# Layer norm's factor as exp(-0.5 ln(var + eps)), with one activation table set for the whole kernel

## Chip, cores, metric

The kernel runs on one core of a Trainium2 chip. The metric is the device time of one execution in microseconds (us), medians of several executions. A trace belongs to one execution; its span is some 1.8 us shorter than the time. A span is printed to 0.1 us, so lengths that run to its end are good to 0.05 us.

## The reference, cut to what matters

```python
def _layernorm(x, axis=-1, eps=1e-5):
    m = jnp.mean(x, axis=axis, keepdims=True)
    v = jnp.var(x, axis=axis, keepdims=True)
    return (x - m) / jnp.sqrt(v + eps)

# x: 64 graphs x 256 nodes x 512 features, adj: 64 x 256 x 256, all float32
x = _layernorm(x + relu(concat([x, adj @ x / deg]) @ W.T))            # layer 0
w = inv_scale * mask * rowsum((x @ Wq) * (adj @ (mask * (x @ Wk))))
x = _layernorm(x + softmax(w, axis=nodes)[:, :, None] * (x @ Wv))     # layer 1
```

Two norms for each graph, 128 in all, and one softmax over the nodes of each graph. The kernel does the softmax for two graphs at once, 32 times.

## The kernel before

The kernel is software-pipelined: round i does layer 0 of graph i, layer 1 of graph i-2, and finishes graph i-4. Its products use a seven-multiplication block scheme; their helper is line L155, the products with the adjacency are L254. A scheduler decides the order on each engine from the program's dependencies and its own estimate of the times, so that a changed instruction can also move others.

```python
    def transpose_rows(src, dst):            # x1 -> x1T, for the products of layer 1
        ...
        for t in range(NT):
            nc.vector.transpose(sq[:, :, :, t, :].rearrange("p b c q -> p c b q"), src[:, t, :])
        ...
        for a in range(P // Q):
            for b in range(P // Q):          # 16 transfers, issued one after the other
                nc.sync.dma_start(to[b * Q:(b + 1) * Q, :, a, :], ...)

    def layer_norm(src, dst):
        mv = small.tile([P, NT, 2], F32, name="mv")
        for t in range(NT):
            st = small.tile([P, 6], F32, name="st")
            nc.vector.bn_stats(st, src[:, t, :])
            nc.vector.bn_aggr(mv[:, t, :], st)
        rstd = small.tile([P, NT], F32, name="rstd")
        nc.scalar.activation(rstd, mv[:, :, 1], AF.Sqrt, bias=eps)      # L180
        nc.vector.reciprocal(rstd, rstd)                                # L181
        for t in range(NT):                                             # L183
            nc.vector.tensor_scalar(dst[:, t, :], src[:, t, :], mv[:, t, 0:1], rstd[:, t:t + 1],
                                    op0=OP.subtract, op1=OP.mult)
    ...
    def norm0(g):                            # end of layer 0
        layer_norm(owns.pop(g), x1s[g])
        for t in range(NT):                  # masked copy for the adjacency product of the next round
            nc.scalar.activation(values(g + 1)[:, 1, t, :], x1s[g][:, t, :], AF.Copy,
                                 scale=mask_sb[:, t, g:g + 1])
        transpose_rows(x1s[g], x1Ts[g])
    ...
    def softmax_rows(k):
        ...
        wr = ps_tp.tile([G, NT, P], F32, name="tp")
        for t in range(NT):
            nc.tensor.transpose(wr[:, t, :], w[:, t, :], ident)         # L349
        nc.vector.reduce_max(top, wr.rearrange("g t p -> g (t p)"), axis=AX.X)
        nc.vector.tensor_scalar(top, top, -1.0, None, op0=OP.mult)      # L352
        nc.scalar.activation(e, wr, AF.Exp, bias=top, accum_out=total)  # L355
        nc.vector.reciprocal(total, total)
        nc.vector.tensor_scalar(e, e, total, None, op0=OP.mult)
        return e
    ...
    def finish(g):
        for t in range(NT):
            nc.vector.scalar_tensor_tensor(o[:, t, :], v[:, t, :], p[:, t, g % G:g % G + 1], x1[:, t, :],
                                           op0=OP.mult, op1=OP.add)     # L371
        layer_norm(o, o)
        nc.sync.dma_start(out[g].rearrange("(t p) f -> p t f", p=P), o)
```

The square root and the exponential lie in different table sets of ScalarE, so each softmax brings two table loads: the exponential's, and the square root's for the next norm. A table load (ACT_TABLE_LOAD) is put in wherever the needed function isn't in the loaded set.

## Time and profile before

| | before |
|---|---|
| median of 3 runs (later, of 6) | 2003.67 us (2003.88 us) |
| span of the profiled run | 2002.7 us |
| TensorE (PE) busy | 1971.7 us, 98% |
| VectorE (DVE) busy | 1526.0 us, 76% |
| ScalarE (ACT) busy | 677.8 us, 34% |
| of that, table loads | 66, of 1.283 us each |
| granted clock of TensorE, mean | 0.995 |

Read it from the top: a kernel whose TensorE is busy for 98% of the span can lose time to another engine only where TensorE waits for it. The prediction shows where that is: at the start, and in the last 60 us, when the pipeline drains and no other graph's work covers a wait.

### The profile page before, as it was taken

The page shows a single profiled execution, that of the slowest core. Times are in us where ns is not written, and L with a number is a line of the kernel's source. Part 1 is how long each engine was busy: PE and PEld are TensorE (multiplying, and loading weights), DVE is VectorE, ACT ScalarE, POOL GpSimd, SP SyncE. Part 2 cuts the span into 40 slices and gives each one's busy share as a digit, 9 for nine tenths or more (in the row PEclk, how much of TensorE's full clock was granted, in tenths as well). Part 3 has the DMA queues.
Part 4 walks back from the last instruction along what each step waited for, and adds up shares of the span by engine and source line. Part 5 has one row for each costly group of instructions (what it writes and reads, how often), then busy time and mean ns, then how long its engine had stood idle before and what let it go on. Part 6 is the DMA issues. An engine that isn't in the chain of part 4 may idle for free.

```text
span 2002.7 us, 19342 instructions
## 1 busy us (share of the span) xinstructions
PE 1971.7 (98%) x5536; PEld 1030.1 (51%) x5536; DVE 1526.0 (76%) x3184; ACT 677.8 (34%) x1354; POOL 418.0 (21%) x518
## 2 busy tenths in 40 slices
PE   8999999999999999999999999999999999999995
PEld 3555555555555555555555555555555555555552
DVE  4677778777788777787777787777877777877776
ACT  2333333333333333333333333333333333333322
POOL 3122122221221221221222212212212212222100
PEclk9999999999999999999999999999999999999998
DMA  6333332333333333333323323323233333233211
GB/s 221 85 79 78 96 90 74 91 89 84 90 79 92 94 75 94 90 75 99 90 76 89 93 78 92 89 82 92 73 95 90 78 96 90 73 91 92 60 38 53
DMA packets 384905, 174.40 MB, mean 87 GB/s; under 512 B 283809, under 2 KB 349473, under 8 KB 384801
## 3 DMA queue, kind: packets, MB, share of 16 engines
q1 hardware_dynamic: 384800, 173.17, 32.6%
q8 instruction: 46, 0.75, 0.2%
q14 instruction: 59, 0.48, 0.1%
HBM read 105.97 MB, written 33.55 MB: 70 GB/s over the span
## 4 chain that ended last, share of the span: by engine, by line
PE 97%; DVE 1%; SPq 0%; ACT 0%; DMA 0%; issue 0%; DVEq 0%; ACTq 0%
PE mm L155 77%; PE mm L254 19%; PE mm L126 1%; SPq L170 0%; PE tp L363 0%; PE tp L349 0%; DMA wqk<-wqk_t 0%; DVE st L177 0%; DVE o L371 0%; ACT L355 0%; DVE own L286 0%; DVE own L288 0%; DMA x1T<-sq 0%; DVE o L183 0%; ACT vals L295 0%
## 5 line engine op out<-in xcount | busy, mean ns | idle before, releaser
L155 PE MATMUL mm<-w,s 128*128 128x512 f32 x1024 | 481.3, 592 | 0.7 <-ACT v L325 0.7
L155 PE MATMUL mm<-t,s 128*128 128x512 f32 x1024 | 464.9, 596 | 0.6 <-ACT q L318 0.6
L155 PEld LDWEIGHTS mm<-t,s 128*128 128x128 f32 x1024 | 192.4, 190 | 231.1 <-issue 214.0
L155 PEld LDWEIGHTS mm<-w,s 128*128 128x128 f32 x1024 | 194.5, 190 | 192.6 <-issue 170.0
L155 PE MATMUL mm<-w,x1T 128*128 128x512 f32 x512 | 242.6, 596 | 4.1 <-DMA x1T<-sq 4.1
L155 PE MATMUL mm<-w,xT 128*128 128x512 f32 x512 | 240.9, 592 | 0.0
L196 POOL TENSOR_TENSOR sa<-adj 128x128 f32<-128x128 f32 x64 | 45.8, 715 | 773.7 <-PE mm L254 772.2
L147 POOL TENSOR_TENSOR s<-xT 128x256 f32<-128x256 f32 x64 | 46.5, 726 | 704.4 <-PE mm L155 684.7
L254 PE MATMUL mm<-tv,sa 128*128 128x256 f32 x768 | 187.4, 379 | 0.6 <-DVE tv L244 0.4
L254 PEld LDWEIGHTS mm<-tv,sa 128*128 128x128 f32 x768 | 145.7, 190 | 76.3 <-issue 60.3
L155 PEld LDWEIGHTS mm<-w,xT 128*128 128x128 f32 x512 | 97.3, 190 | 94.7 <-issue 91.3
L333 DVE TENSOR_TENSOR v<-mm,v 128x512 f32<-128x512 f32 x64 | 44.2, 691 | 127.5 <-ACT v L332 127.5
L286 DVE SCALAR_TENSOR_TENSOR own<-zr,rdeg,own 128x512 f32<-128x512 f32 x128 | 107.6, 841 | 42.4 <-ACT zr L276 42.4
L155 PEld LDWEIGHTS mm<-w,x1T 128*128 128x128 f32 x512 | 95.3, 191 | 86.0 <-issue 74.8
L325 ACT COPY v<-mm 128x512 f32<-128x512 f32 x64 | 37.4, 585 | 299.6 <-PE mm L155 299.6
L314 DVE SCALAR_TENSOR_TENSOR q<-mm,zr 128x512 f32<-128x512 f32 x128 | 87.6, 684 | 66.7 <-PE mm L155 66.6
L155 PE MATMUL mm<-t,x1T 128*128 128x512 f32 x256 | 125.5, 612 | 0.7 <-ACT v L332 0.7
L254 PE MATMUL mm<-vals,adj 128*128 128x256 f32 x512 | 121.3, 379 | 1.9 <-DVE vals L228 1.9
L155 PE MATMUL mm<-t,xT 128*128 128x512 f32 x256 | 120.5, 593 | 2.4 <-ACT vals L217 2.4
L371 DVE SCALAR_TENSOR_TENSOR o<-v,probs,x 128x512 f32<-128x512 f32 x128 | 120.2, 958 | 0.1
L254 PEld LDWEIGHTS mm<-vals,adj 128*128 128x128 f32 x512 | 97.1, 190 | 43.6 <-issue 20.8
L210 ACT COPY own<-mm 128x512 f32<-128x512 f32 x64 | 37.4, 585 | 227.5 <-PE mm L155 227.5
(83 smaller groups left out, 2676.4 us busy)
## 6 DMA issues: line engine op xcount, KB each, us to landing
xT<-x_t SPq DMA_DIRECT2D x64, 512.0 KB, 4.3
x<-x SPq DMA_DIRECT2D x64, 512.0 KB, 3.6
x1T<-sq SPq DMA_DIRECT2D x1024, 32.0 KB, 2.0
out<-o SPq DMA_DIRECT2D x64, 512.0 KB, 2.9
adj<-adj_t SPq DMA_DIRECT2D x64, 256.0 KB, 2.7
rows<-adj SPq DMA_DIRECT2D x64, 256.0 KB, 4.9
wqk<-wqk_t SPq DMA_DIRECT2D x4, 512.0 KB, 5.2
w<-w_t SPq DMA_DIRECT2D x4, 512.0 KB, 9.2
```

Of the source, the lines that this page charges most:

```text
L126: nc.tensor.matmul(ps[c], wqk[:, a, c * P:(c + 1) * P], wqk[:, NA + a, :], start=(a == 0), stop=(a == NA - 1))
L147: eng.tensor_add(s1, a21, a22)
L155: nc.tensor.matmul(ps, a[:, c, :], b[:, c, :], start=start and c == 0, stop=(c == H - 1), skip_group_check=True)
L196: nc.gpsimd.tensor_add(sa[:, 0], a21, a22)
L210: began = nc.scalar.copy(own[:, 0, :], u)
L254: nc.tensor.matmul(ps[:, k * HF:(k + 1) * HF], sumsA[g - k][a], w[b][:, n, :], start=start and n == 0, stop=True, skip_group_check=True)
L286: nc.vector.scalar_tensor_tensor(own[:, t, :], z[:, t, :], rdeg[:, t:t + 1], own[:, t, :], op0=OP.mult, op1=OP.add)
L314: nc.vector.scalar_tensor_tensor(q, a, 1.0, agg[:, t, :], op0=OP.mult, op1=OP.mult, accum_out=to)
L325: nc.scalar.copy(v[:, 0, :], u)
L333: nc.vector.tensor_add(v[:, 1, :], p5, v[:, 1, :])
L371: nc.vector.scalar_tensor_tensor(o[:, t, :], v[:, t, :], p[:, t, g % G:g % G + 1], x1[:, t, :], op0=OP.mult, op1=OP.add)
```

## The change

The intent: get rid of all table loads but one, and of the reciprocals. 1/sqrt(v) is exp(-0.5 ln v), and one table set holds both ln and exp. It is loaded at the start and serves the softmax too.

```diff
+    nc.scalar.preload_act_table_set("natural_log_exp_and_others")
     const = ctx.enter_context(tc.tile_pool(name="const", bufs=1))
@@ layer_norm
-        nc.scalar.activation(rstd, mv[:, :, 1], AF.Sqrt, bias=eps)
-        nc.vector.reciprocal(rstd, rstd)
+        nc.scalar.activation(rstd, mv[:, :, 1], AF.Ln, bias=eps)
+        nc.scalar.activation(rstd, rstd, AF.Exp, scale=-0.5)
```

From here on, a line number of the changed kernel is larger by one than that of the kernel before (L156 for L155); the experiments' own edits shift theirs a little more.

## The prediction

> **What bounds the kernel now.** I read the page first (share of the span of each engine), then the chain that ended last, then the waits of TensorE, then the busy time by stretch, and last the timeline of the tail.
>
> ```profile
> PE 1971.7 (98%) x5536; PEld 1030.1 (51%) x5536; DVE 1526.0 (76%) x3184; ACT 677.8 (34%) x1354; POOL 418.0 (21%) x518
> ...
> PE 97%; DVE 1%; SPq 0%; ACT 0%; DMA 0%; issue 0%; DVEq 0%; ACTq 0%
> ```
>
> TensorE (PE) is busy for 1971.7 of 2002.7 us, and the chain is 97% matmuls. Only 31 us of the span are not matmuls; nothing that leaves the matmuls alone can win more than that. The waits of TensorE say where these 31 us lie (us in total, times, longest):
>
> ```profile
> PE mm L126 <- DMA wqk<-wqk_t: 4.5, 1, 4.5
> PE mm L155 <- DMA x1T<-sq: 4.1, 1, 4.1
> PE tp L363 <- DVE e L357: 3.6, 1, 3.6
> PE mm L155 <- ACT vals L217: 2.4, 2, 1.7
> ...
> PE mm L155 <- ACT v L325: 0.7, 1, 0.7
> PE mm L155 <- ACT v L332: 0.7, 1, 0.7
> PE mm L155 <- ACT q L318: 0.6, 1, 0.6
> ```
>
> Nearly every one happens once, so they belong to the start and the tail, not to the 64 rounds. The stretches confirm it (window, its length, then busy time of PE, PEld, DVE, ACT, POOL, then granted clock and DMA):
>
> ```profile
> 62.62:1944.19 1881.57, 1881.57 (x5309) 986.80 (x5309) 1458.12 (x3042) 644.40 (x1286) 400.47 (x488) 1.00 0.33 85
> ```
>
> From 62.62 to 1944.19 us TensorE is busy all 1881.57 us at full clock. The layer norms in there can't be seen in the time.
>
> What the change touches, from the groups of instructions:
>
> ```profile
> L180 ACT ACT_TABLE_LOAD x33 | 42.3, 1283 | 0.6
> L355 ACT ACT_TABLE_LOAD x32 | 41.1, 1283 | 34.4 <-DVE top L352 34.4
> L180 ACT ACTIVATE rstd<-mv,eps 128x2 f32<-128x2 f32 x128 | 37.8, 295 | 95.7 <-DVE mv L178 94.3
> L181 DVE RECIPROCAL rstd<-rstd 128x2 f32<-128x2 f32 x128 | 19.4, 151 | 8.0 <-ACT rstd L180 8.0
> ```
>
> Each softmax (L355, one per two graphs) loads the exponential's table and the next norm (L180) loads the square root's back: 65 loads, 83.4 us of ScalarE, plus one at the very start. It looks like 4% of the span, but ScalarE is 34% busy and waits mostly for TensorE.
>
> **What the Trainium skill says.** "ScalarE: Activation LUTs", section "What ACT_TABLE_LOAD costs": about 1283 ns per load, the same for every set, and about 1380 ns of drain at each switch. The trace agrees on 1283 ns; it shows no drain as a gap: in the last softmax the load starts at 1987.92, and the exponential at 1989.22, 0.02 us after it ends. I count 1.28 us per load. Section "Table sets: the hidden batching unit" of that page: exp and ln are together in natural_log_exp_and_others, so one load serves both. The trace before can't show that; the changed program, built and listed, holds one load in place of 66. The page's cost of an ACTIVATE (186 ns with immediate scale and bias, 93 ns for each pointer operand, 0.83 ns per element) makes the new Exp on 2 columns 0.19 us, 0.28 if the zero bias goes by pointer; the trace has 0.295 for the Sqrt with a pointer bias, so I use 0.2 to 0.3. "TensorE: Matmul & The Clock Gate", section "What's actually happening": the array falls to half clock after an idle window of some 3.4 us. The trace agrees: in the one wait for x1T in the tail the clock drops, and the next 3.5 us run at 0.50:
>
> ```profile
> 1966.90:1970.99 4.09, 0.00 (x1) 0.03 (x1) 3.23 (x10) 0.29 (x1) 0.00 (x0) 0.77 0.39 91
> 1970.99:1974.50 3.51, 3.51 (x4) 1.48 (x5) 1.49 (x4) 0.00 (x0) 0.00 (x0) 0.50 0.67 247
> 1974.50:1978.60 4.10, 4.10 (x9) 1.81 (x8) 0.70 (x2) 0.59 (x1) 0.00 (x0) 0.83 0.00 0
> ```
>
> **The change part by part, middle.** Removed: 65 loads (83.4 us of ACT) and 128 reciprocals (19.4 us of DVE). Added: 128 Exp on ACT (26 to 38 us, an estimate from the 0.2 to 0.3 us above). Ln takes Sqrt's place at the same 0.295 us. So ACT should fall from 678 to 622 to 634 us and DVE from 1526 to about 1507. I compared the two built programs. TensorE's order is the same but for a handful of matmuls in the last rounds; GpSimd's is the same. On VectorE the steady order moves a little: one pair of output scalings (L183, 1.0 us) now precedes the add that frees a PSUM bank (L265), where a reciprocal and two other additions stood. Nothing here precedes a matmul that waits. Worth in the middle: 0 us. At the start (45 to 50 us) the first load ends at 46.69, before its statistics are there (mv at 46.82), so it is hidden: 0 us.
>
> **The tail, where it can count.** Two places have a load on the path.
>
> First, the softmax at 1951 us. The load of 1.28 us holds the copy of q, the next load holds the norm of the last graph, and this norm decides when x1T starts to be transposed:
>
> ```profile
> 1951.30 1.28 ACT L355 ACT_TABLE_LOAD   x1 [3.83 <-DVE top L352]
> ...
> 1953.64 1.28 ACT L180 ACT_TABLE_LOAD   x1
> 1953.67 1.12 PE L155 MATMUL mm<-t,s 128*128 128x512 f32 x2 [0.59 <-ACT q L318]
> ...
> 1956.64 1.00 DVE L183 TENSOR_SCALAR x<-own,mv,rstd 128x512 f32<-128x512 f32 x2
> ...
> 1958.91 10.40 SPq L170 DMA_DIRECT2D x1T<-sq  x16
> ```
>
> With the order of the changed program I replay it with these durations. The exponential runs at 1951.26 and is read out by 1951.9; statistics (L177, L178) and the small softmax product end at about 1953.95; Ln and Exp take 0.6 us to 1954.6, beside the dot product of 0.75 us that VectorE does meanwhile; L183 starts at 1954.75, not 1956.64: 1.9 us earlier. The 16 transposing transfers start 1.9 us after that start, are issued serially in 10.4 us, and TensorE waited 4.09 us for the last. It therefore resumes 1.9 us earlier, at about 1969.1. Gain 1.9 us.
>
> TensorE's own work before it starts about when it did (1956.7, now waiting for the masked copy) and ends near 1966.7, so its wait shrinks to 2.2 to 2.6 us. In the trace before, a mean clock of 0.77 over 4.09 us, if it was first 1.00 and then 0.50, means that the clock fell 2.2 us into the wait. So it is even whether the shorter wait still costs the half clock. If not, the 4 matmuls take 1.88 and the next 8 take 3.60 in place of 3.75 and 4.28: 2.5 us. At even odds I count 1.3 us.
>
> Second, the last softmax: its load (1987.92, 1.28 us) stands between the maximum and the exponential with nothing beside it. Gain 1.28 us. The load after it is hidden: the last norms' Sqrt starts at 1994.51, as soon as its statistics are there.
>
> Given back: at the very end the changed order scales the graph before the last before it takes the last statistics; the last Ln and Exp are then exposed, 0.6 us, where before the scaling covered Sqrt and reciprocal. The first of the two outputs leaves earlier and doesn't share the DMA with the last: 0.1 us back.
>
> Sum: 1.9 + 1.3 + 1.28 - 0.6 + 0.1 = 4.0 us. 2003.7 - 4.0 = 1999.7 us.
>
> **The rivals.** (a) The loads count in full: 83 us of ACT less 32 of Exp, so some 50 us and 1953 us, if ScalarE paced the rounds. Against it: the stretch of 1881.57 us without a gap, and TensorE's busy time of 1971.7 us, that is not touched. I give it 1%. (b) A new wait takes their place: Ln and Exp now stand in ScalarE's in-order queue ahead of a PSUM copy, and the L183 pair delays L265. Each round two copies are close: the matmul after L332's copy starts as soon as it ends. Should a round lose 0.3 us, it would be 64 x 0.3 = 19 us, 2019 us. Against it: Ln and Exp take 0.6 us where load and Sqrt took 1.58, and where no load was they take 0.3 more, with the copy's wait for TensorE mostly above 0.8 us. 4%. (c) The tail's gain is hidden: TensorE or VectorE, not x1T, ends the wait, as VectorE is over 90% busy there. Then only the 1.28 - 0.6 us of the end remain: 2003 us. 20%. (d) My replay with the cold clock kept: 2001.0; with it warm: 1998.5.
>
> **Range and chances.** From (d), with 1.5 us for the spread of the three runs before (2001.9 to 2005.0), and (c) at its upper end: 1997.0 to 2002.8. 2% is 40 us, more than all of the time that isn't matmuls: faster 0.01, slower 0.01, within 0.98.
>
> **What would show it.** One load in the list of groups; ACT near 628, DVE near 1507, PE within 3 us of 1971.7 unless the tail's clock stays up; the middle still without a wait; L183 of the last graph starting some 1.9 us nearer to the start of its softmax; a wait for x1T of 2 to 3 us; the last exponential directly after L352. Wrong: a wait of TensorE for ACT or DVE that comes some 30 or 60 times, or a wait for x1T that is unchanged.

## The result

| | before | after |
|---|---|---|
| median (lowest to highest), 6 runs each | 2003.88 (2001.94 to 2004.99) us | 2000.26 (1998.14 to 2002.65) us |
| span of the profiled run | 2002.7 us | 1996.4 us |
| TensorE busy | 1971.7 us | 1968.4 us |
| VectorE busy | 1526.0 us | 1514.0 us |
| ScalarE busy | 677.8 us | 628.1 us |

The ratio is 0.9984 (95% interval 0.9971 to 0.9996). A ratio is the mean time of one kernel's fast runs over that of the other's of the same rounds, so it is not quite the ratio of the medians. The change is real and small: 3.6 us between the medians, of 85 us of table loads. The profiled run of the changed kernel happens to be its fastest of six, and that of the kernel before (2004.58 us) is slower than its median, so the two traces lie further apart (6.3 us) than the medians.

The page of the changed kernel, and its groups that answer to the four shown before (count, then busy us and mean ns, then idle time ahead):

```profile
PE 1968.4 (99%) x5536; PEld 1029.0 (52%) x5536; DVE 1514.0 (76%) x3056; ACT 628.1 (31%) x1417; POOL 411.1 (21%) x518
...
L181 ACT ACTIVATE rstd<-mv,eps 128x2 f32<-128x2 f32 x128 | 37.8, 295 | 110.8 <-DVE mv L179 108.1
L182 ACT ACTIVATE rstd<-rstd 128x2 f32<-128x2 f32 x128 | 26.0, 203 | 4.0
...
L69 ACT ACT_TABLE_LOAD x1 | 1.3, 1283 | 0.7 <-PEq L431 0.7
```

One load is left; the new Exp takes 203 ns. ScalarE lost 49.7 us of work, and the time fell by 3.6. The same stretch in the middle as before, and TensorE's waits within it (us, times, longest):

```profile
62.62:1944.19 1881.57, 1881.06 (x5307) 986.71 (x5306) 1446.22 (x2918) 600.47 (x1348) 392.19 (x486) 1.00 0.33 85
...
PE mm L156 <- ACT vals L218: 0.5, 1, 0.5
```

Before, TensorE was busy for all of this stretch; now it waits once, for 0.5 us. So nothing was won in the middle. What is left is the start and the tail. I cut the span at events that all versions share:

- start: the first product of layer 0 begins at 20.96 us before and at 20.14 after. In eleven traces it begins between 19.99 and 21.23 us, in no relation to the edits, which leave the matmuls ahead of it as they are. I don't credit these 0.8 us to the change.
- middle: from there to the last regular product (`mm<-t,x1T`, at 1944.03 and 1943.46 us), 1923.07 us before and 1923.32 after: 0.25 us lost.
- tail: from there to the end, 58.67 us before and 52.94 after: 5.73 us won.

The tail by sections, in us:

| section of the tail | before | after | difference |
|---|---|---|---|
| (1) to the first matmul after the wait for x1T | 26.96 | 24.74 | -2.22 |
| (2) to the transposes of the last scores (L349) | 15.47 | 13.03 | -2.44 |
| (3) to the first product with the last softmax (L371) | 4.59 | 3.23 | -1.36 |
| (4) to the last pair of scalings (L183) | 6.47 | 7.03 | +0.56 |
| (5) to the end of the span | 5.18 | 4.91 | -0.27 |

The timeline of the changed kernel in section (1) (start, duration, engine, line; in brackets the idle time ahead and what ended it):

```profile
1950.75 0.47 ACT L356 ACTIVATE e<-tp,top 2x256 f32<-2x256 f32 x1 [3.84 <-DVE top L353]
...
1953.12 0.29 ACT L181 ACTIVATE rstd<-mv,eps 128x2 f32<-128x2 f32 x1 [1.35 <-DVE mv L179]
...
1953.44 0.20 ACT L182 ACTIVATE rstd<-rstd 128x2 f32<-128x2 f32 x1
...
1953.68 1.00 DVE L184 TENSOR_SCALAR x<-own,mv,rstd 128x512 f32<-128x512 f32 x2
...
1955.96 10.39 SPq L171 DMA_DIRECT2D x1T<-sq  x16
...
1968.20 1.96 PE L156 MATMUL mm<-w,x1T 128*128 128x512 f32 x4 [2.31 <-DMA x1T<-sq]
```

The exponential starts without a load ahead of it, the norm's factor follows as soon as its statistics are there, and the last graph is scaled 10.22 us after the last regular product (1953.68 - 1943.46); before, it was 12.61 (1956.64 - 1944.03). The transposing transfers start as much earlier, and TensorE's wait for them shrinks from 4.09 to 2.31 us. After it the four matmuls take 1.96 us, where they took 3.75 at half clock.

Not all of these 2.39 us can be put down to the loads. The same place in the kernel before, from the square root on:

```profile
1954.93 0.30 ACT L180 ACTIVATE rstd<-mv,eps 128x2 f32<-128x2 f32 x1
...
1955.24 0.75 DVE L371 SCALAR_TENSOR_TENSOR o<-v,probs,x 128x512 f32<-128x512 f32 x1
1955.91 0.16 DVE L181 RECIPROCAL rstd<-rstd 128x2 f32<-128x2 f32 x1
1955.99 0.73 DVE L371 SCALAR_TENSOR_TENSOR o<-v,probs,x 128x512 f32<-128x512 f32 x1
```

ScalarE was done with the square root 11.20 us after the last regular product (1955.23 - 1944.03), and is done with Exp after 10.18 (1953.64 - 1943.46): 1.02 us. The other 1.37 us lie on VectorE. From there to the start of the scaling 1.41 us passed before, with the reciprocal between two instructions that finish an earlier graph (L371), and 0.04 us after, where those two (L372) come behind the scaling. Loads, reciprocal and order changed together, and no run parts them.

Section (3), the timeline of the kernel before and that of the changed one:

```profile
1987.70 0.14 DVE L352 TENSOR_SCALAR top<-top 2x1 f32<-2x1 f32 x1
1987.92 1.28 ACT L355 ACT_TABLE_LOAD   x1 [5.06 <-DVE top L352]
1989.22 0.46 ACT L355 ACTIVATE e<-tp,top 2x256 f32<-2x256 f32 x1
```

```profile
1982.47 0.14 DVE L353 TENSOR_SCALAR top<-top 2x1 f32<-2x1 f32 x1
1982.71 0.46 ACT L356 ACTIVATE e<-tp,top 2x256 f32<-2x256 f32 x1 [5.07 <-DVE top L353]
```

The load's place is simply gone. Section (4), from the chain that ended last in the changed kernel (start, duration, what):

```profile
1990.67 0.23 DVE mv L179 x2
1990.90 0.02 issue
1990.92 0.30 ACT rstd L181
1991.23 0.02 issue
1991.25 0.21 ACT rstd L182
1991.46 0.03 issue
1991.49 0.55 DVE o L184
```

Statistics, Ln, Exp and the scaling follow each other with nothing beside them. That is the half microsecond that was given back.

### The profile page after: what moved, and what is told of

It is laid out like the page before. It is cut to its first block, busy times and chain, and to the rows that moved or that the text cites. A ratio compares the mean times of both kernels' runs of the same rounds, so it can differ in the third digit from the quotient of the medians.

```text
span 1996.4 us, 19070 instructions
## 1 busy us (share of the span) xinstructions
PE 1968.4 (99%) x5536; PEld 1029.0 (52%) x5536; DVE 1514.0 (76%) x3056; ACT 628.1 (31%) x1417; POOL 411.1 (21%) x518
## 4 chain that ended last, share of the span: by engine, by line
PE 96%; DVE 2%; SPq 1%; DMA 0%; ACT 0%; issue 0%; DVEq 0%; ACTq 0%
PE mm L156 76%; PE mm L255 19%; SPq L171 1%; PE mm L127 1%; PE tp L364 0%; PE tp L350 0%; DVE st L178 0%; DMA xT<-x_t 0%; DMA wqk<-wqk_t 0%; DVE own L289 0%; DVE own L287 0%; DVE o L372 0%; ACT vals L296 0%; DVE x L184 0%; DMA x1T<-sq 0%
## 5 line engine op out<-in xcount | busy, mean ns | idle before, releaser
L156 PE MATMUL mm<-w,s 128*128 128x512 f32 x1024 | 481.2, 592 | 0.0
L156 PE MATMUL mm<-t,s 128*128 128x512 f32 x1024 | 463.9, 595 | 0.0
L156 PEld LDWEIGHTS mm<-t,s 128*128 128x128 f32 x1024 | 192.1, 190 | 229.2 <-issue 213.6
L156 PEld LDWEIGHTS mm<-w,s 128*128 128x128 f32 x1024 | 194.6, 190 | 191.1 <-issue 162.6
L156 PE MATMUL mm<-w,x1T 128*128 128x512 f32 x512 | 240.8, 593 | 2.3 <-DMA x1T<-sq 2.3
L156 PE MATMUL mm<-w,xT 128*128 128x512 f32 x512 | 240.9, 592 | 0.0
L229 DVE TENSOR_TENSOR vals<-mm,vals 128x512 f32<-128x512 f32 x64 | 44.3, 692 | 134.6 <-PE mm L156 134.6
L156 PEld LDWEIGHTS mm<-w,xT 128*128 128x128 f32 x512 | 97.3, 190 | 94.6 <-issue 91.3
L156 PEld LDWEIGHTS mm<-w,x1T 128*128 128x128 f32 x512 | 94.8, 190 | 83.7 <-issue 79.4
L156 PE MATMUL mm<-t,x1T 128*128 128x512 f32 x256 | 125.5, 612 | 0.9 <-ACT v L333 0.7
L156 PE MATMUL mm<-t,xT 128*128 128x512 f32 x256 | 120.6, 593 | 2.8 <-ACT vals L218 2.8
L372 DVE SCALAR_TENSOR_TENSOR o<-v,probs,x 128x512 f32<-128x512 f32 x128 | 118.4, 963 | 0.0
```

Of the source, the lines that this page charges most:

```text
L156: nc.tensor.matmul(ps, a[:, c, :], b[:, c, :], start=start and c == 0, stop=(c == H - 1), skip_group_check=True)
L229: nc.vector.tensor_add(y[:, 0, :], p5, y[:, 0, :])
```

## The experiments

Theory: the gain lies in the tail alone, in three terms (the last graph's norm earlier, TensorE's clock, the last softmax's load), less what the exposed Ln and Exp at the end give back. Rivals: the middle's relief of ScalarE and VectorE brings it; the clock isn't the cause of the slow matmuls; the spread is all there is to see. All results were correct against the reference. All were timed in 5 rounds but for the last, in 3; the kernel before ran along, with medians of 2004.21, 2003.51 and 2003.15 us in the three sessions.

### Ln and Exp in the tail alone, and in the middle alone

```diff
-        nc.scalar.activation(rstd, mv[:, :, 1], AF.Ln, bias=eps)
-        nc.scalar.activation(rstd, rstd, AF.Exp, scale=-0.5)
+        if at_round[0] >= 62:              # tail_only;  < 62 in middle_only
+            nc.scalar.activation(rstd, mv[:, :, 1], AF.Ln, bias=eps)
+            nc.scalar.activation(rstd, rstd, AF.Exp, scale=-0.5)
+        else:
+            nc.scalar.activation(rstd, mv[:, :, 1], AF.Sqrt, bias=eps)
+            nc.vector.reciprocal(rstd, rstd)
```

(In tail_only the shared set is loaded ahead of the exponential of round 62, in middle_only at the start.)

> Ln and Exp with the shared set only from round 62 on (the last softmax but one, the norms of the last graphs); square root, reciprocal and 61 loads in all rounds before. My theory (the gain lies in the tail alone): the tail from the last regular rounds to the end takes about 53 us as in the changed kernel, not 58.7 as in the kernel before, the middle keeps its loads and shows no wait, and the time is within 1.5 us of the changed kernel's 2000.3. Rival (the middle's relief of ScalarE and VectorE brings the gain): the time stays at that of the kernel before, 2003.9.

> The complement: Ln and Exp with the shared set up to round 61, square root, reciprocal and five loads from round 62 on. My theory: 60 loads and over 110 reciprocals less in the middle bring nothing; the tail takes about 58.7 us as before, and the time is 2003.9 within 1.5 us (or 0.5 to 0.8 us worse, for the one new wait of TensorE for the copy to vals near 70 us). Rival: most of the gain of 3.6 us is here, about 2000.5.

Measured: tail_only 1998.29 us (1997.40 to 2000.24), ratio to before 0.9972 (0.9959 to 0.9984). middle_only 2004.38 us (2003.11 to 2005.38), ratio 1.0001 (0.9988 to 1.0013). The tail takes 52.94 us in tail_only, as in the changed kernel, and 60.08 in middle_only. The stretch from 62.62 us to the last regular product, first in tail_only, then in middle_only (columns as before: PE, PEld, DVE, ACT, POOL, then clock and DMA):

```profile
62.62:1943.46 1880.84, 1880.84 (x5308) 986.19 (x5306) 1458.93 (x3038) 644.26 (x1287) 398.35 (x487) 1.00 0.33 85
```

```profile
62.62:1943.32 1880.70, 1880.19 (x5306) 985.61 (x5304) 1445.20 (x2921) 601.43 (x1345) 397.47 (x486) 1.00 0.33 85
```

With all its loads and 43 us more of ScalarE's work, tail_only's TensorE never waits in the middle; relieved, that of middle_only waits the same 0.5 us as in the changed kernel. The rival falls: 59 loads and over 110 reciprocals less in the middle gain nothing, and the new order costs a little there. (tail_only's 2 us below the changed kernel's median of six is more than the middle explains; it is outside the 1.5 us that I expected. They ran on different occasions, and I take no more from it than that it isn't slower.)

### The clock: the wait filled with useless matmuls

```diff
+        if i == B + 1:
+            warm = bank()
+            for _ in range(4):
+                nc.tensor.matmul(warm, ident, w0[:, 0, :], start=True, stop=True, skip_group_check=True)
         l1 = layer1_steps(i - 2) if 0 <= i - 2 < B else iter(())
```

> The kernel before with four useless matmuls (about 3.4 us) that run in the tail's wait for x1T. My theory (2.4 us of the changed kernel's gain is TensorE's clock, which no longer falls to half because the wait is short): from the first matmul after the wait to the transposes of the last scores 13.0 us, not 15.5, granted clock 1.00 there, nothing else moves, 2001.5 us. Rival (those 12 matmuls are slow for another reason, such as the row sums or the transfers): 15.5 us stay, 2003.9 us.

Measured: 2002.63 us (2002.26 to 2005.56), ratio 0.9995 (0.9982 to 1.0009), so the time alone would not settle it. The sections do: 27.97, 13.03, 4.60, 6.46 and 5.11 us. Section (2) is 13.03 us, to the hundredth that of the changed kernel, with the same norms and loads as before:

```profile
1966.33 3.60 PE L400 MATMUL mm<-w,ident 128*128 128x512 f32 x8
1971.60 1.96 PE L155 MATMUL mm<-w,x1T 128*128 128x512 f32 x4 [1.68 <-DMA x1T<-sq]
```

The matmuls after the wait take 1.96 us. That the 2.44 us of section (2) are the clock's is shown, and the rival falls. Section (1) was 1 us longer here than in the profiled run of before. It is 27.6 to 28.0 us in the three other traces with the old tail, and 24.7 to 25.6 in the traces with the new one: the 16 transfers' issue takes 10.4 to 11.4 us from one execution to the next. The profiled run of before was a lucky one in this section. Why the issue varies stays open.

### The last load alone

```diff
+        if k == B // G - 1:
+            tc.keep_in_program_order(nc.scalar.preload_act_table_set("exp_and_others"))
         wr = ps_tp.tile([G, NT, P], F32, name="tp")
```

> The kernel before with the exponential's table for the very last softmax loaded some 4 us earlier, while ScalarE is idle; every load is still there. My theory (of 65 loads this is one of the two that cost): from the transposes of the last scores to the first product with the softmax 3.3 us, not 4.6; all else as before; 2002.6 us. Rival (the load there is hidden by the read-out and the waits around it): 4.6 us stay.

Measured: 2002.19 us (2001.42 to 2003.44), ratio 0.9991 (0.9979 to 1.0004). Section (3) is 3.23 us, as in the changed kernel, where it was 4.59. The timeline of this kernel:

```profile
1982.53 1.28 ACT L348 ACT_TABLE_LOAD   x1
...
1987.58 0.46 ACT L357 ACTIVATE e<-tp,top 2x256 f32<-2x256 f32 x1 [3.77 <-DVE top L354]
```

The same load, five microseconds earlier, is free. It is its place that cost 1.36 us. Not all else was as before, though: section (2) took 14.73 us in place of 15.47, since the clock was at half for 3.41 us and not for 6.83. So the sections show the load's cost; the 2.0 us between the medians hold more than the load, and the interval of the ratio reaches beyond 1.

### The changed kernel again, and with the last scalings held back

> The changed kernel once more, on the chip of the next two. 2000 us within 1.5; the tail 52.9 us when the clock stays up and about 55.4 when it falls; again one wait of 0.5 us near 70 us that the kernel with Ln and Exp in the tail alone hasn't.

Measured: 1999.23 us (1998.93 to 2000.30), ratio 0.9980 (0.9967 to 0.9992); tail 53.89 us, sections 25.62, 13.03, 3.32, 7.03, 4.89. The wait for x1T was 3.19 us here, and the clock held. From the first product to the last regular one it took 1923.75 us. In the five traces with Ln and Exp from the start on this is 1923.32 to 1923.77 us; in the six with the old rounds it is 1923.06 or 1923.07 in five, and 1922.62 in one.

For end_order the statistics and the scaling of a norm were made separate functions, and `finish` uses them:

```diff
-        layer_norm(o, o)
-        nc.sync.dma_start(out[g].rearrange("(t p) f -> p t f", p=P), o)
+        mv = small.tile([P, NT, 2], F32, name="mv")
+        stats(o, mv)
+        held.append((g, o, mv, factor(mv)))       # factor: Ln and Exp
+        if g == B - 2:
+            return
+        for h, o, mv, rstd in held:
+            scaled(o, o, mv, rstd)
+            nc.sync.dma_start(out[h].rearrange("(t p) f -> p t f", p=P), o)
+        held.clear()
```

> The changed kernel, with the scaling of the last two graphs held back until both have their statistics, so that other work covers the last Ln and Exp, as the kernel before covered its last square root. My theory (0.56 us were given back because the last Ln and Exp stand exposed): from the first product with the last softmax to the last scaling 6.2 to 6.5 us, not 7.0, and 0.6 us less in all, or a little less because both outputs then leave together. Rival (the last stretch is bound by VectorE's own work or the output's transfer): no change in the span.

Measured: sections (4) and (5) 6.45 and 5.14 us, against 7.03 and 4.91. So the 0.56 us are the exposed pair's, as expected, and 0.23 us go back, probably because both outputs leave together. But the time was 2002.54 us (1998.30 to 2003.10), in two clumps: 1998.3 and 1999.4, and 2002.5 to 2003.1. The mean clocks fit them: 0.997 in the two short runs, 0.996 in the three long ones. The profiled run is of the second clump, and the stretches show why (the last three columns are granted clock, DMA share and GB/s):

```profile
1966.00:1969.00 3.00, 1.09 (x4) 0.38 (x2) 2.83 (x7) 0.10 (x1) 0.00 (x0) 1.00 0.28 45
1969.00:1973.00 4.00, 3.04 (x4) 1.51 (x5) 2.43 (x6) 0.39 (x2) 0.00 (x0) 0.52 0.74 269
```

After a wait of 2.87 us the clock fell to half, and section (2) took 16.02 us. So the changed kernel's tail draws lots in each execution: the clock held after waits of 2.31 and 3.19 us, and fell after one of 2.87. What the lots are, the next section shows.

### Two versions meant to be better, and the lots taken away

The first has square root, reciprocal and loads up to round 61 (tail_only), and the held-back scalings.

> A version meant to beat both: square root, reciprocal and loads up to round 61, Ln and Exp from round 62 (which showed no new wait in the middle), and the last scalings held back. 0.6 us less than with Ln and Exp in the tail alone: tail 52.3 us, 1998 us.

Measured: 2000.26 us (1999.36 to 2001.30), ratio 0.9984 (0.9971 to 0.9996). A miss. The wait was 2.30 us, and the clock fell all the same (section (2) 14.73 us), which outweighs the 0.3 us of the scalings. But that is not the whole of it: the profiled run is the fastest of the five, and the two slowest (2000.47 and 2001.30 us) have a mean clock of 0.997, as the runs with a warm tail have. What made those slow stays open.

In tail_only the wait was 2.30 us as well, and the clock held. The record of the granted clock in the traces shows the difference. In all twelve traces the clock changes only at the ends of steps of 3.413 us, counted from its first rise, and each stretch at half clock in between lasts a whole number of steps (3.41 us in the run both, 6.83 in the kernel before). How the steps lie against the work differs from one execution to the next. Two steps of the run both, then two of tail_only (`prof both --windows 1965.17:1968.59,1968.59:1972.00`, and likewise; columns as before):

```profile
1965.17:1968.59 3.42, 1.12 (x5) 0.51 (x4) 2.79 (x8) 0.50 (x2) 0.00 (x0) 1.00 0.55 167
1968.59:1972.00 3.41, 3.41 (x6) 1.33 (x5) 2.02 (x7) 0.59 (x1) 0.00 (x0) 0.50 0.48 175
```

```profile
1964.03:1967.44 3.41, 1.86 (x6) 0.74 (x4) 3.41 (x8) 0.12 (x1) 0.00 (x0) 1.00 0.31 51
1967.44:1970.86 3.42, 2.67 (x7) 1.26 (x8) 2.67 (x9) 1.08 (x3) 0.00 (x0) 1.00 0.62 232
```

In the run both, the wait (1965.74 to 1968.04) lies within one step, and TensorE is busy for 1.12 us of it. In tail_only a step ends inside the wait (1965.89 to 1968.19), and TensorE is busy for 1.86 and 2.67 us of the two. In the eleven traces without no_preload all 16 falls from full to half clock follow a step with TensorE busy for 1.36 us or less, and no step with 1.45 us or more is followed by one. no_preload blurs the edge a little: 21 of its 22 falls follow a step of at most 1.44 us and one a step of 1.74, and one step of 1.41 has no fall. So it isn't the length of the wait that decides, but how much work the step around it holds. This is read from the traces; no run moved the steps on purpose. A fall doesn't cost a fixed amount either: section (2) took 14.73, 15.47, 16.02 or 16.04 us with one, and 13.03 or 13.04 without.

The other two have three filling matmuls in the tail, one in after_warm's changed kernel and one in the version above.

> The changed kernel with three useless matmuls in the tail (one where TensorE waits for a copy anyway, two in its wait of 2.3 to 3.2 us for x1T). My theory: the half clock after that wait comes in some executions and not in others, which spreads the changed kernel's times by 2.5 us; with the wait filled it never comes: 13.0 us from the end of the wait to the last scores, times close together near 1999, and none of the 2001 to 2003 that the changed kernel and the one with the held-back scalings showed. Rival: the spread is of the start (the first 16 us of matmuls, 15.5 to 16.8 us long) and stays.

> A version meant to beat both kernels: Ln and Exp from round 62 only, the last scalings held back, and the same three useless matmuls. Tail 52.3 to 53 us in every run, 1998 to 1998.5 us.

Measured: after_warm 1999.54 us (1998.94 to 1999.86), ratio 0.9981 (0.9968 to 0.9993). both_warm 1998.47 us (1998.19 to 1999.20), ratio 0.9975 (0.9962 to 0.9989). Section (2) is 13.03 and 13.04 us. The five times lie within 0.92 and 1.01 us; without the filling they lay within 4.5 us (the changed kernel's six), 1.4 (its five in after_again), 2.8 (tail_only), 4.8 (end_order) and 1.9 (both). With the filling, the steps in and next to the wait hold 2.61 us of TensorE's work or more. That the times above 2001 us are the clock's is likely for end_order, whose mean clocks fit, and not shown for the rest: of the changed kernel's three such times one, 2001.51 us, has the same mean clock of 0.997 as the fast ones. both_warm has the lower median of the two. It beats the kernel before by 4.7 us of medians in its session, and after_warm, the changed kernel with the same filling, by 1.1. Its tail took 53.10 us, 0.1 above the expected 52.3 to 53, and two of its five times lie above the expected 1998 to 1998.5 us.

### Far more loads

The changed kernel without its first line: the scheduler's own placing gives each norm a load for Ln and one for Exp, 257 in all.

```diff
-    nc.scalar.preload_act_table_set("natural_log_exp_and_others")
```

> The changed kernel without the shared set: every norm loads the logarithm's table and then the exponential's, 257 loads in all. How far does the middle hide loads? ScalarE rises from 628 to about 957 us, 48% of the span. If its share alone counted, all would stay hidden and only the tail would lose: about 2006 us. My theory: a load costs when it stands in ScalarE's in-order queue ahead of a copy that TensorE needs soon. In the built order two norms stand back to back ahead of such a copy every second round (6.2 us where 1 was, some 3 us late), one norm in the other rounds (3.1 us, some 2.5 us late): 64 times about 2.5 us, roughly 2160 us (2050 to 2250), with TensorE waiting for the copies to vals.

Measured: 2190.18 us (2183.37 to 2191.70), ratio 1.0920 (1.0904 to 1.0937). TensorE's waits and the timeline of ScalarE in one of the rounds with two norms:

```profile
PE mm L156 <- ACT vals L218: 109.2, 33, 3.5
PE mm L156 <- ACT vals L214: 25.2, 31, 0.8
```

```profile
966.11 1.28 ACT L181 ACT_TABLE_LOAD   x1
967.40 0.29 ACT L181 ACTIVATE rstd<-mv,eps 128x2 f32<-128x2 f32 x1
967.72 1.28 ACT L182 ACT_TABLE_LOAD   x1
969.01 0.20 ACT L182 ACTIVATE rstd<-rstd 128x2 f32<-128x2 f32 x1
969.23 1.28 ACT L181 ACT_TABLE_LOAD   x1
...
973.47 0.56 ACT L218 COPY vals<-mm 128x512 f32<-128x512 f32 x1
```

ScalarE is busy for 947 us, 43% of the span, and yet it holds TensorE up: the copy to vals stands behind four loads in a row (the fourth is left out here) and the masked copies. With the two norms of every second round, 33 waits make 109 us; the others make 25, less than my 2.5 us each. Beside these waits of 134 us the matmuls themselves grew by 57 us (2025.6 us busy, mean clock 0.978): I had left out that each wait may bring slow matmuls with it. A share of 34 or 43% says nothing of whether a load is hidden; what stands behind it in the queue does.

## Why the prediction was right

It was right in time (1999.7 us predicted; 2000.26 and 1999.23 us measured) and in its mechanism, with three terms mis-sized. That it came within 0.6 us is in part luck: the clock's term was the mean of two outcomes, and a fall of the clock cost between 1.70 and 3.01 us.

- **The middle is worth nothing.** Right: middle_only has a ratio of 1.0001. Rival (b), a new wait, came true once instead of 64 times: 0.5 us near 70 us, where the scheduler put the masked copies ahead of a copy that TensorE needs. The time from the first product to the last regular one is longer by 0.25 to 0.7 us with it. The prediction's "nothing here precedes a matmul that waits" was too strong by that; it had compared VectorE's order in the steady rounds, and the wait lies on ScalarE in round 1.
- **The norm of the last graph 1.9 us earlier.** Right in kind; it was 2.39 us, of which 1.02 lie on ScalarE and 1.37 in VectorE's new order, which the replay took from the changed program. So calling it a load on the path tells only part. The replay set the statistics and the small product at 9.92 us after the last regular product; Ln began at 9.66. I had added durations of instructions whose records overlap by up to 0.1 us each, which may be why. The scaling, and with it the transfers, came 0.5 us earlier than replayed. The transfers begin 2.27 us after the start of the scaling (1958.91 - 1956.64), not 1.9 as the prediction read; its sum uses only the shift.
- **The clock, 2.5 us at even odds.** The size fits these two traces (2.44 us, and in before_warm the same without any other edit), by luck, as a fall cost between 1.70 us (both) and 3.01 (middle_only). The odds fit too: in the five traces with the new tail and no filling it held in three (after, after_again, tail_only) and fell in two (end_order, both). The argument for them failed. The clock did fall 2.2 us into the wait before (1969.07 against 1966.90), but there a step ended in which TensorE had been busy for 1.24 us; with the new tail it fell with waits of 2.30 and 2.87 us and held with 2.30 and 3.19. So the trace of the kernel before agreed with an idle window of some 3.4 us only in part: the clock fell too early for it.
- **The last load, 1.28 us.** 1.36 us, shown by before_prefetch alone.
- **Given back, 0.6 us.** 0.56 us, and end_order takes it back.
- **The output, 0.1 us.** 0.27 us.
- **The sum.** Predicted 4.0 us with half of the clock's term; the two traces' tails differ by 5.73 us with all of it, and would by 3.3 without. Less 0.25 us in the middle, the medians' 3.6 and 4.3 us lie between.
- **Busy times.** ACT 628.1 us lies in the predicted 622 to 634, by luck: the terms give 620 to 632 (677.8 - 83.4 + 26 to 38), and with the Exp's measured 26.0 us 620.4. VectorE was put at 1507 us and is 1514.0. Busy time counts overlapping records once, and the reciprocals overlap their neighbours: taken out of the trace of the kernel before, their 19.4 us lower VectorE's busy time by 9.4 only. Beside that, the gather's first subtraction (L244, now L245) rose by 7.6 us in all and its last (L247, now L248) fell by 6.5. Why was not tested.

Rival (a) would have needed TensorE to wait in the rounds; rival (c), the wait ending with something other than x1T, didn't come: the wait still ended with x1T.

## What to carry to other kernels

Count the table loads that stand in front of something the busiest engine waits for, not the loads. Here 3 of 66 do, all where the pipeline drains and nothing else is left to do; for the last a run shows its cost (1.36 us), for the two ahead of the last graph's norm their share isn't parted from VectorE's order. A load that does stand in the way can be put a few microseconds earlier, where its engine is idle, which gained as much in that place as doing without it. When the edit is worth a few microseconds, cut the traces of both kernels at events that they share, and look at TensorE's granted clock around each wait, step by step, before believing a difference of medians.

## What the Trainium skill lacked or had wrong

- "ScalarE: Activation LUTs", section "What ACT_TABLE_LOAD costs": the 1283 ns are right, but the 1380 ns of drain added to every switch were not there to be saved. Where a load lay bare, taking it away gained 1.36 us (4.59 to 3.23 us), and moving it earlier gained the same; the sum of 2.66 us is about twice that. In no_preload, too, a load starts 0.03 us after the ACTIVATE ahead of it ends (967.69 to 967.72 us).
- The same page tells what a load costs and to batch by set, but not when it counts: 59 loads fewer in rounds bound by TensorE gained nothing (2004.38 against 2004.21 us), while 257 loads, with ScalarE busy for 43% of the span, cost 187 us; 109 of the 134 us of waits stood behind four loads in a row ahead of one copy.
- The same page's cost of an ACTIVATE with immediate scale and bias, 186 ns + 0.83 ns per element, comes near: 203 ns for 2 columns, where the estimate from it is 188. Ln or Sqrt with a pointer bias took 295 ns, where the estimate from its formula is 282.
- "TensorE: Matmul & The Clock Gate", section "What's actually happening": the idle window of some 3.4 us need not be idle, and the page doesn't say how little work will do. The clock fell after steps of 3.41 us with up to 1.36 us of matmuls in them, at waits of 2.30 and 2.87 us, and held after steps with 1.45 us or more, at a wait of 3.19 us too (eleven traces; no_preload blurs the edge). That the window runs free, as the page says, agrees with the traces: all changes of the clock lie whole steps of 3.413 us apart. Three filling matmuls cut the wait to 0.8 us, and the clock held in both traces.
